# A vision stack on one Trainium2 core: transposes and projections of a chunked scan in one matmul per half

## The chip, the cores and the metric

The kernel runs on one core of a Trainium2 chip. The time is the device time of that core, in microseconds (us), for one execution over a batch of eight images. The engines have these names: PE (TensorE) multiplies matrices and writes to PSUM, with its weight loads shown apart as PEld; DVE (VectorE), ACT (ScalarE) and POOL (GpSimd) work on elements; SP issues DMAs. [...]

## The reference, cut to what matters

The input is x of shape (8, 64, 64, 96). Four layers follow each other, each adding its output to its input: three state-space blocks (layers 0, 1 and 2) and a spectral layer. The change lies in layer 1. There the normalised input is projected to 192 inner channels, passed through a 3x3 depthwise convolution and silu (call the result u), and scanned in K = 4 directions: rows, columns, and both reversed. For every direction k and every position, a projection of u gives 6 values of dt, 16 of B and 16 of C. The scan goes by chunks:

```python
x_dbl = jnp.einsum('blkd,kcd->blkc', xs, x_proj_w)
dts, Bs, Cs = jnp.split(x_dbl, [R, R + D_STATE], axis=3)
dt = jax.nn.softplus(dts + dtb)
S_loc = jnp.einsum('bcsh,bcshn,bcshd->bchdn', decay_end * dtr, Brh, xr)
```

Here `xr` is u with positions first. So the chunked scan needs u, dt and B with positions on the partitions, where the convolution leaves u with channels on the partitions. Every value is fp32.

## The kernel before, in words

The images go one after the other. For each, `u` and `y` lie in SBUF as two halves of 96 channels, each with L = 4096 positions. Layer 1 is `chunked_scan`, which calls `chunked_order` (L744) twice: order 0 for rows (directions 0 and 2), order 1 for columns (directions 1 and 3). A call has two parts.

The first part is a block whose order of work on each engine is set by the Tile planner, from its own costs and the order of the source. In order 0 it begins with the convolution (L766 to L774), which is mostly DVE's work (L256, L258) with a last block on PE (L269); POOL scales the identity for that (L263). Then PE computes B and C of all positions with channels on the partitions (L782), DVE copies them out (L790) and SP writes them to memory (L793). Then comes the loop over NQ = 32 chunks of Q = 128 positions (L796 to L820). In order 1 a chunk of u is a strided view, so POOL and ACT first copy the two halves to `uc` (L802, L803), which has four buffers. For each half, PE transposes the 96 x 128 piece into the PSUM tile `pt`, two buffers (L807); ACT for even chunks and DVE for odd ones copies it to `xt` (L808). PE then multiplies the same two pieces with the projection's columns for dt and B of both directions, 2 x 22 = 44 columns, adding up the halves in the PSUM tile `px`, which holds four chunks in one buffer (L812); DVE copies it to `xd` every fourth chunk (L820). In both kinds of PE work the piece of u is the stationary operand, loaded as 128 columns. After the loop, DVE adds the bias to dt (L824), ACT takes softplus (L829), DVE multiplies by A (L834), PE sums along the chunk (L839), ACT takes exp (L840), and DVE forms `d_end` (L841). Each of these works on all chunks at once.

The second part, the main part, is the scan itself in an order written out by hand (L1064 to L1085), a step for every two chunks. It begins with the DMA loads of `bt` and `cr` on SP's queue (L863, L867) and PE's `pl` (L872), and its matmuls into `py` (L1022, L1030) are the last that it issues. Its tiles take over memory from those of the first part.

## Time and profile before

| what | value |
|---|---|
| median of 3 runs | 31217.13 us (31208.32 to 31267.33) |
| profiled execution | 31126.95 us, its span 31125.2 us |
| PE, weight loads | 24477.4 us (79%), 9300.6 us (30%) |
| DVE | 24790.2 us (80%) |
| ACT | 16342.4 us (53%) |
| POOL | 21609.0 us (69%) |
| mean granted TensorE clock | 0.732 |

A line of the groups reads: source line, engine, operation, tile written and tiles read, partitions x elements, count; then total busy us and mean ns of one; then the engine's idle us just before these instructions, and what ended it. A line of the timeline reads: start, length in us, engine, line, operation, how many were merged. A line of the stretches is explained where it stands. L numbers are lines of the kernel before. "PEclk" or the granted clock is the share of full speed at which TensorE was let run.

### The profile page before, as it was taken

Reading aid. Unit: us, or ns where it says so; the run is one execution under the profiler, and the core shown is the slowest. Engines: PE = TensorE matmul, PEld = TensorE weight load, DVE = VectorE, ACT = ScalarE, POOL = GpSimd, SP = SyncE. Lnnn points to the kernel's source line nnn. Section 1 sums busy time; section 2 is a strip of 40 time slices with the busy share of each in tenths; the row PEclk is TensorE's granted clock in tenths of the full one; section 3 lists DMA queues with packets and bytes.
Section 4 is the critical chain, followed back from the end, with each engine's and each line's share of the span. In section 5 each row is a group of like instructions: output and inputs, shape, how many; then the busy total and the mean of one; then the engine's idle time right before and its main releaser. Section 6 shows DMA issues by size and latency. Waiting matters only on the chain. (4 is left out here: it accounts for less than half of the span.)

```text
span 31125.2 us, 279248 instructions
## 1 busy us (share of the span) xinstructions
PE 24477.4 (79%) x90246; PEld 9300.6 (30%) x90246; DVE 24790.2 (80%) x17921; ACT 16342.4 (53%) x28493; POOL 21609.0 (69%) x8844
## 2 busy tenths in 40 slices
PE   7797877978779787797877978779787797877978
PEld 1241422414225132241412414124141241412414
DVE  9859688596885968859698596985969859698596
ACT  5536455364553645536455364653646536465364
POOL 8739487395873958739587394973948739487394
PEclk7777776777777777777777777777777777776777
DMA  5315253052530525305253152531525315253152
GB/s 124 90 24 131 64 120 92 23 133 64 119 93 21 131 67 120 92 23 132 64 122 89 25 132 63 123 88 28 133 59 123 88 27 132 60 123 88 27 132 62
DMA packets 1503971, 2689.39 MB, mean 86 GB/s; under 512 B 305624, under 2 KB 313144, under 8 KB 1502512
## 3 DMA queue, kind: packets, MB, share of 16 engines
q1 hardware_dynamic: 1485872, 2665.23, 36.6%
q8 instruction: 722, 11.83, 0.2%
q10 hardware_dynamic: 16640, 6.29, 0.1%
q14 instruction: 737, 6.04, 0.1%
HBM read 2287.51 MB, written 383.06 MB: 86 GB/s over the span
## 5 line engine op out<-in xcount | busy, mean ns | idle before, releaser
L569 DVE TENSOR_TENSOR_SCAN h<-da,db 128x1026 f32<-128x1026 f32 x6144 | 13727.8, 2280 | 513.0 <-PE py L607 173.9
L590 POOL TENSOR_TENSOR h<-h,c 128x2048 f32<-128x2048 f32 x3072 | 12755.2, 4183 | 148.4 <-ACT state L585 144.5
L533 PE MATMUL pu<-du,cst 32*128 32x512 f32 x4096 | 3239.1, 881 | 3525.3 <-DVE db L539 3493.7
L554 ACT ACTIVATE da<-dx,a0s 128x512 f32<-128x512 f32 x6144 | 4235.3, 690 | 2600.4 <-DVE h L569 2440.4
L554 ACT ACTIVATE da<-dx,a2s 128x512 f32<-128x512 f32 x6144 | 4234.5, 690 | 2591.4 <-DVE h L569 2432.0
L607 PE MATMUL py<-h,cst 128*32 128x512 f32 x24576 | 5432.2, 814 | 68.3 <-POOL h L590 68.0
L539 POOL TENSOR_TENSOR db<-du,b 128x2048 f32<-128x2048 f32 x1024 | 4657.7, 4549 | 580.8 <-ACT db L525 580.8
L539 DVE TENSOR_TENSOR db<-pu,b 128x2048 f32<-128x2048 f32 x2048 | 4637.4, 2264 | 6.3 <-issue 6.3
L607 PEld LDWEIGHTS py<-h,cst 128*32 128x32 f32 x24576 | 1182.6, 145 | 4982.1 <-issue 4505.5
L533 PEld LDWEIGHTS pu<-du,cst 32*128 32x128 f32 x4096 | 802.3, 243 | 5542.4 <-DVE db L539 3998.6
L229 POOL TENSOR_SCALAR xn<-xs,sb 96x512 f32<-96x512 f32 x192 | 208.0, 1088 | 3179.8 <-DVE sb L209 3038.8
L455 PE MATMUL pv<-u,wk 96*128 96x512 f32 x2048 | 1765.1, 1003 | 759.0 <-ACT raw L451 759.0
L952 ACT ACTIVATE sg<-sg 128x768 f32<-128x768 f32 x1024 | 819.2, 800 | 2422.4 <-PE sg L936 2422.4
L883 POOL TENSOR_TENSOR rr<-lr,cc 128x768 f32<-128x768 f32 x256 | 435.9, 1703 | 2266.9 <-ACT lr L881 1177.4
L446 PE MATMUL pv<-u,wk 96*96 96x512 f32 x2048 | 1475.4, 849 | 501.1 <-ACT state L585 239.4
L597 PE MATMUL py<-y,cst 96*96 96x512 f32 x1536 | 1551.2, 1108 | 394.6 <-ACT raw L460 356.7
L498 POOL TENSOR_TENSOR du<-raw,u 96x512 f32<-96x512 f32 x1024 | 1445.7, 1438 | 0.0
L984 DVE TENSOR_TENSOR wt<-wt,cbm 128x768 f32<-128x768 f32 x1024 | 1091.0, 1085 | 344.5 <-ACT wt L953 341.2
L585 ACT COPY state<-h 128x4 f32<-128x4 f32 x3072 | 604.6, 197 | 1163.9 <-DVE h L569 1163.8
L1022 PE MATMUL py<-wt,xdt 128*32 128x128 f32 x12288 | 1017.0, 331 | 233.2 <-DVE y L1060 155.0
L1146 DVE SCALAR_TENSOR_TENSOR f<-p,w3bs,f 128x512 f32<-128x512 f32 x768 | 576.4, 751 | 718.6 <-ACT f L1139 691.8
L1030 PE MATMUL py<-ce,state 96*96 96x128 f32 x3968 | 1115.4, 371 | 0.0
(210 smaller groups left out, 32236.4 us busy)
## 6 DMA issues: line engine op xcount, KB each, us to landing
dx<-dd SPq DMA_DIRECT2D x4096, 192.0 KB, 3.8
b<-bcd SPq DMA_DIRECT2D x2048, 256.0 KB, 5.2
c<-bcd SPq DMA_DIRECT2D x2048, 256.0 KB, 6.5
du<-dud SPq DMA_DIRECT2D x2048, 128.0 KB, 2.7
dd<-raw SPq DMA_DIRECT2D x1024, 192.0 KB, 5.3
dud<-du SPq DMA_DIRECT2D x512, 128.0 KB, 1.9
xd<-xs SPq DMA_DIRECT2D x256, 192.0 KB, 2.1
xs<-xd SPq DMA_DIRECT2D x128, 384.0 KB, 5.8
```

What stands on the lines that cost most here:

```text
L446: nc.tensor.matmul(pv[:DM], weights[k][:, hi, 128:], uv[hi], start=(hi == 0), stop=(hi == 1))
L455: nc.tensor.matmul(pv, weights[k][:, hi, :128], uv[hi], start=(hi == 0), stop=(hi == 1))
L498: nc.gpsimd.tensor_mul(cut(du[:, hf, :], wh), cut(delta[hf], wh), uv[hf])
L533: nc.tensor.matmul(pu, sel[rows, :], m["du"][rows, n // 3, :], start=True, stop=True)
L539: (nc.gpsimd if pool else nc.vector).tensor_mul(groups(m["db", n]), (m["du2"][:, n // 3, :] if pool else m["pu"]) .unsqueeze(1) .to_broadc ...
L554: nc.scalar.activation(dst[:, g, :LC], made[i]["dx"][n // 3][:, n % 3, :], AF.Exp, scale=av4[:, k, n, gs : gs + 1],)
L569: nc.vector.tensor_tensor_scan(made[i]["h", n][:, at][:, way], das[p][:, rev : 2 * SEG + rev][:, way], made[i]["db", n][:, at][:, way], 0. ...
L590: nc.gpsimd.tensor_mul(h, h, made[i]["c"])
L597: nc.tensor.matmul(py, skip[:, hf, :] if k == 0 else ident[:DM, :DM], view((u if k == 0 else y)[:, hf, :], wh, c * LC, LC), start=True, st ...
L607: nc.tensor.matmul(py[32 * q : 32 * q + 32, :], red, hs[q][:, g, :], start=False, stop=(g == NSG - 1),)
L984: nc.vector.tensor_mul(it["wt"], it["wt"], m["cbm"][:, j : j + 1, :].to_broadcast([128, RK, Q]),)
L1030: nc.tensor.matmul(py[:, i, hf, :], it["before"][:, 96 * hf : 96 * hf + 96], m["ce"][:, j, :], start=False, stop=True,)
```

## The change

In the loop over chunks, each half of a chunk gets one matmul in place of a transpose and a projection matmul. Its moving operand `tx` holds, side by side, the 96 x 96 identity and that half's 44 columns of the projection: 140 columns. POOL builds `tx` once per order, in four copies. The result goes to a PSUM tile `pt` of 2 x 140 columns[...], with three buffers; `px` is gone. The transposed piece is copied to `xt` as before, from two runs of 96 columns. The two halves of dt and B are no longer added in PSUM: ACT copies the first half's 44 columns to `xd`, and DVE adds the second half's, for every chunk.

```diff
+        TX = DM + 2 * (RK + NST)
...
-            tc.tile_pool(name="pt", bufs=2, space=PSUM) as ptp,
-            tc.tile_pool(name="px", bufs=1, space=PSUM) as pxp,
+            tc.tile_pool(name="pt", bufs=3, space=PSUM) as ptp,
...
+            tx = cp.tile([DM, 2, TX], F32, name="tx", bufs=1)
+            for hf in range(2):
+                nc.gpsimd.tensor_copy(tx[:, hf, :DM], ident[:DM, :DM])
+                nc.gpsimd.tensor_copy(
+                    tx[:, hf, DM:].rearrange("p (i r) -> p i r", i=2),
+                    xproj[:, o::2, hf, : RK + NST],
+                )
...
-                pt = ptp.tile([128, 192], F32, name="pt")
+                pt = ptp.tile([128, 2, TX], F32, name="pt")
                 for hf in range(2):
-                    nc.tensor.transpose(pt[:, hf * 96 : hf * 96 + 96], uv[hf], ident[:DM, :DM])
-                (nc.vector.tensor_copy if c % 2 else nc.scalar.copy)(xt[:, c, :], pt)
-                if c % 4 == 0:
-                    px = pxp.tile([128, 4, 2, RK + NST], F32, name="px")
-                for hf in range(2):
-                    nc.tensor.matmul(
-                        px[:, c % 4, :, :],
-                        uv[hf],
-                        xproj[:, o::2, hf, : RK + NST],
-                        start=(hf == 0),
-                        stop=(hf == 1),
-                    )
-                if c % 4 == 3:
-                    nc.vector.tensor_copy(xd[:, c - 3 : c + 1, :, :], px)
+                    nc.tensor.matmul(pt[:, hf, :], uv[hf], tx[:, hf, :], start=True, stop=True)
+                (nc.vector.tensor_copy if c % 2 else nc.scalar.copy)(
+                    xt[:, c, :].rearrange("p (j m) -> p j m", j=2), pt[:, :, :DM]
+                )
+                xdc = xd[:, c, :, :].rearrange("p i r -> p (i r)")
+                nc.scalar.copy(xdc, pt[:, 0, DM:])
+                nc.vector.tensor_add(xdc, xdc, pt[:, 1, DM:])
```

## The prediction

> **What bounds the kernel now.** I read the engine table first: PE 79%, DVE 80% and POOL 69% of the span, so no one engine bounds the whole, and the change touches one stage: the loop over 32 chunks that precedes the chunked scan's main part. It runs twice per image (order 0 over rows, order 1 over columns), 16 times in the span. The groups show its members:

> ```profile
> L812 PE MATMUL px<-w1s,uc 96*128 96x44 f32 x1024 | 215.4, 373 | 0.0
> L812 PEld LDWEIGHTS px<-w1s,uc 96*128 96x128 f32 x1024 | 214.8, 302 | 0.0
> L807 PEld LDWEIGHTS pt<-cst,uc 96*128 96x128 f32 x512 | 102.5, 245 | 46.6 <-POOL uc L802 32.8 <-issue 13.5
> L803 ACT COPY uc<-u 96x128 f32<-96x128 f32 x256 | 119.7, 482 | 183.5 <-PE px L812 111.3 <-PE py L1030 67.9 <-PE pt L807 0.7
> L808 DVE COPY xt<-pt 128x192 f32<-128x192 f32 x256 | 90.6, 356 | 418.9 <-PE pt L807 418.4
> L808 ACT COPY xt<-pt 128x192 f32<-128x192 f32 x256 | 80.6, 315 | 347.2 <-PE pt L807 340.0 <-issue 7.3
> L820 DVE COPY xd<-px 128x176 f32<-128x176 f32 x128 | 43.4, 339 | 37.9 <-PE px L812 37.3
> ```

> The reader is to see that everybody waits for PE here, and that one fp32 matmul is two records (1,024 for 512 matmuls) where a transpose is one. So a chunk has six weight loads of 128 columns: two for transposes, four for px. Then busy time by stretches of the first image: the conv before the loop, order 0's loop in three pieces, order 1's in two, then three stretches of the spectral layer:

> ```profile
> 1425.00:1434.40 9.40, 9.40 (x27) 3.15 (x26) 9.40 (x9) 3.44 (x4) 0.82 (x1) 1.00 0.01 2
> 1489.06:1495.09 6.03, 5.78 (x55) 5.25 (x53) 2.65 (x8) 1.59 (x5) 0.00 (x0) 1.00 0.10 26
> 1495.09:1506.48 11.39, 11.21 (x58) 10.62 (x59) 2.34 (x7) 1.28 (x4) 0.00 (x0) 0.51 0.24 58
> 1506.48:1517.00 10.52, 10.34 (x54) 9.76 (x55) 2.11 (x6) 1.59 (x5) 0.00 (x0) 0.50 0.00 0
> 1800.20:1807.06 6.86, 5.86 (x55) 5.39 (x53) 2.83 (x8) 4.89 (x13) 3.64 (x8) 0.92 0.15 39
> 1807.06:1818.90 11.84, 11.30 (x57) 10.78 (x58) 2.85 (x8) 5.06 (x13) 4.08 (x9) 0.50 0.10 26
> 3600.00:3605.00 5.00, 5.00 (x26) 5.00 (x25) 1.70 (x2) 1.29 (x2) 0.00 (x0) 0.50 0.00 0
> 3700.00:3740.00 40.00, 39.94 (x235) 29.15 (x234) 17.74 (x26) 17.57 (x25) 0.00 (x0) 1.00 0.00 1
> 3860.00:3880.00 20.00, 20.00 (x94) 20.00 (x94) 2.46 (x3) 3.07 (x3) 0.00 (x0) 0.50 0.00 1
> ```

> Columns: length, then busy us of PE, weight loads, DVE, ACT, POOL, then the granted clock. Weight loads fill 90% of the loop, ACT and DVE are a quarter busy (ACT 43% in order 1), and about 6 us into the loop the clock falls from 1.00 to 0.50 and stays there. The timeline gives the periods:

> ```profile
> 1501.59 1.01 PEld L812 LDWEIGHTS px<-w1s,u 96*128 96x128 f32 x4
> 1504.64 1.89 PEld L812 LDWEIGHTS px<-w1s,u 96*128 96x128 f32 x8
> 1506.26 0.37 PEld L807 LDWEIGHTS pt<-cst,u 96*128 96x128 f32 x1
> ```

> Four chunks repeat from a load like the last line at 1501.38 to this one: 4.89 us, 1.22 us a chunk. At clock 1.00 it was 0.59 (loads at 1489.57 and 1490.16). Order 1 takes 0.65 a chunk early and 1.26 late. From the first transpose after the bcd matmuls to the last xd copy, the trace's starts and ends give 29.9 to 30.8 us in order 0, mean 30.2 (28 chunks; four run earlier, under the conv), and 36.6 in order 1 (32 chunks): 8 x 66.8 = 534 us, 1.7% of the span. Nothing runs beside it: dt, softplus, pe and d_end need all of xd, the main part needs them.

> [...] 64x64 weights streaming without a pause (L1116, at 3600) got 0.50, 128x128 weights with 64 moving columns per load of 128 (L1169, at 3860) 0.50, but the conv's 96x96 weights without a pause (L269, at 1425) 1.00: as shares of the array at work an estimated 25%, 50% and 56%. The loop now: four matmuls of 44 columns against six loads of 128, well below. [...] the px loads are 0.11 us apart at full clock, 0.21 at half[...]

> **The change, part by part.** Removed per chunk: two transposes and two px matmuls, six loads. Added: two matmuls, four records, each 128 columns loaded and 140 moving. In the conv, records of 504 columns follow each other every 0.42 us at full clock, 0.833 ns a column: 140 x 0.833 = 0.117 us, just over the 0.111 of a load, which therefore hides, as loads do in the conv. PE per chunk: 4 x 0.117 = 0.47 us at full clock (was 0.59), 0.93 at half (was 1.22). The activity becomes 96 of 128 rows x nearly all the time, about 70%: above the conv, so I expect full clock where PE sets the pace.

> Evacuation: the xt copy stays (ACT 0.315 or DVE 0.356, though its source is now two runs of 96). Added is an ACT copy of 44 columns: not in the trace; bounded by ACT's 4-column state copy (0.197) and 192 columns (0.315): I take 0.22. And a DVE add of 44: 176 and 512 columns cost 0.339 and 0.683, so 0.16 + 44 x 1.02 ns = 0.20. Gone is DVE's 0.339 per four chunks. Sums per chunk: ACT 0.38, DVE 0.38, below PE. But the steps form a chain: matmuls 0.47 and 0.2 until the last has drained (a record of 0.286 against a spacing of 0.11), xt copy 0.32 or 0.36, xd copy 0.22 [...], add 0.20, four hand-overs at an estimated 0.07 (DVE's dt add to ACT's softplus took 0.04): 1.7 us. Three pt buffers make 0.57 a chunk. The floor is PE's 0.47; if ACT and DVE, in order, take turns (xt, xd, add, xt, xd: 0.32 + 0.22 + 0.20 + 0.36 + 0.22 = 1.32 for two chunks), 0.66. I take 0.62. In order 1 ACT also has the uc copy (0.447 apart when back to back): 0.447 + 0.38 = 0.83, below PE at half clock (0.93); at this pace the activity is near 40%, so half clock will come and go. Bounds 0.72 (ACT's copies overlap at their ends, as an xt and a uc copy started 0.22 apart now) to 1.1 (both uc copies inside the turns: (1.32 + 0.89)/2); I take 0.93.

> Early chunks: with every chunk needing a DVE add, and DVE in the conv until 1484, three pt buffers allow three instead of four. Order 0: 29 x 0.62 + 1.0 to drain = 19.0, against 30.2: -11.2. Order 1: 32 x 0.93 + 1.2 = 31.0 against 36.6: -5.6. Tail: the Softplus table load (1.28 us) sits behind ACT's last copy; it was issued at 1517.02 and hidden by PE (DVE's xd copy ended at 1518.91). Now ACT's last copy comes 0.2 before the add, and add plus two dt adds (0.82) cover it only in part: +0.5 per order. Sum: (-11.2 - 5.6 + 1.0) x 8 = -126 us.

> At nothing: tx, four POOL copies an order (an estimated 1.5 us by L802's 0.46 for 128 columns). In order 1 POOL is free at 1788.2 and the first transpose comes at 1800.2, after 12 us of bcd matmuls; the uc copies queued behind tx need 2.1. In order 0 it queues behind lw's copy, which ends at 1425.8, 8 us before the first chunk. Without that cover: 1.5 x 16 = 24 us. tx also holds its memory to the last matmul; if cr comes to lie there, order 0's cr DMAs move from 1497 to the loop's end, with bt's later ones behind them on SP. Order 1 has that already (cr at 1836.46), and its end-of-xd to d_end takes the same 6.4 us: nothing.

> The profiled execution took 31126.95 (span 31125.2), 90 below the median shown, 31217.13. The difference goes on the median: 31217 - 126 = 31091.

> **Rivals.** *Half clock stays*: 29 x 0.93 + 1.0, less the 6 us at full clock that the entry gives (about 6 x 0.46/0.47 = 6) = 22; order 1 32 x 0.95 + 1.2 = 31.6: (-8.2 - 5.0 + 1.0) x 8 = -98, 31119. For it: the present loop; against: the conv at 1.00. *The main part's clock moves*: from d_end to the last py matmul, order 0 takes 249.6 to 262.4 (mean 256.9), order 1 283.0 to 293.4 (mean 289.4), for equal work, by where half-clock stretches fall. If a shifted start gave all the long values: 5.5 x 8 + 4.0 x 8 = +76, total -50, 31167; all the short: -58 - 51 = -109, 30982. Nothing in the profile says which. *ACT pairs well in order 1* (0.72): 24.2, -12.4 instead of -5.6: -180, 31037. *Slower: the chain is not overlapped*. If the planner's order leaves one pt in flight (ACT's next copy queued behind one that waits for DVE), 1.7 us a chunk: 29 x 1.7 = 49 and 32 x 1.7 = 54, +19 and +18, x 8 = +296, 31513. It decides from 1.03 us a chunk in order 0 and 1.12 in order 1. Against it: ACT, DVE and POOL run ahead freely now, and three buffers have to be lost, not one.

> **How the numbers follow.** Forecast 0.45; half clock 0.17; good pairing or short main parts 0.15; long main parts or a slower order that eat the gain to within 62 us 0.14; chain serial, wholly or enough to lose, 0.09. A measurement tells about 0.2%, 62 us, from no change. Faster by more: nearly all of the first three, 0.75; same 0.15; slower 0.10. The range takes in good pairing with short main parts in one order, -225 (30990), and the half clock with long main parts, near -25 (31190); the likeliest case alone is 31040 to 31140.

> **What would show it.** PE's loop records: four of 96x140 per chunk, loads hidden. Clock near 1.00 in order 0's loop (else the half-clock rival). Loop lengths near 19 and 31 us. ACT's 44-column copy near 0.22, DVE's add near 0.20, with waits on each other; if PE waits for DVE's add longer than 0.5 us a chunk, the serial rival holds. The prediction is wrong if the 16 main parts change by more than the loops, or if the conv gets longer because adds are slotted into it.

## The result and the profile after

The changed kernel takes 30914.5 us in the median (30896.96 to 31024.2) beside 31208.32 us before: a ratio of 0.9913, 95% interval 0.989 to 0.9936. Measured again beside the experiments, it was 30943.04 against 31163.21, ratio 0.9934 (0.992 to 0.9949). So it is faster by about 0.7 to 0.9%, some 220 to 294 us. The profiled executions differ by 230 us (span 31125.2 before, 30895.2 after). The forecast was 126 us, its range began at 30990, and both measurements lie below it.

The groups of the loop in the changed kernel, in the columns used before (L815 is now the matmul, L816 the xt copy, L820 and L821 the copy and the add to xd, L810 ACT's uc copy):

```profile
L815 PE MATMUL pt<-tx,uc 96*128 96x140 f32 x1024 | 147.2, 292 | 17.2 <-DVE xd L821 16.7
L815 PEld LDWEIGHTS pt<-tx,uc 96*128 96x128 f32 x1024 | 129.6, 189 | 46.6 <-POOL uc L809 26.9 <-issue 16.6
L810 ACT COPY uc<-u 96x128 f32<-96x128 f32 x256 | 101.3, 450 | 69.2 <-PE py L1031 69.2
L821 DVE TENSOR_TENSOR xd<-xd,pt 128x44 f32<-128x44 f32 x512 | 92.6, 198 | 177.4 <-ACT xd L820 101.1 <-PE pt L815 45.4 <-POOL uc L809 27.7
L820 ACT COPY xd<-pt 128x44 f32<-128x44 f32 x512 | 91.2, 203 | 75.4 <-DVE xt L816 75.4
L816 DVE COPY xt<-pt 128x192 f32<-128x192 f32 x256 | 89.9, 351 | 16.5 <-PE pt L815 16.5
```

Four weight loads a chunk are left, and their mean fell from the 302 ns of px's loads to 189 at the same 128 columns. That goes with the clock: in the kernel before, px's loads were 0.11 us apart at 1.00 and 0.21 at 0.50. PE now waits a little for DVE's add (17 us in all), and ACT's 44-column copy for DVE's xt copy of the same pt (75 us). The stretches of the two loops of the first image, in the columns explained before, two lines of the kernel before and two of the changed kernel:

```profile
1489.06:1518.95 29.89, 28.88 (x170) 27.01 (x168) 7.81 (x23) 5.75 (x15) 0.00 (x0) 0.61 0.11 27
1800.21:1836.74 36.53, 33.78 (x195) 31.84 (x192) 9.56 (x26) 17.96 (x45) 12.72 (x28) 0.58 0.06 16
1491.80:1510.80 19.00, 16.11 (x118) 14.64 (x116) 9.90 (x46) 8.29 (x44) 0.00 (x0) 1.00 0.13 31
1797.60:1819.10 21.50, 18.36 (x131) 16.18 (x128) 10.61 (x50) 17.43 (x77) 11.99 (x28) 1.00 0.06 15
```

In the changed kernel the clock is 1.00 through both loops, in all eight images, where its mean had been near 0.60 and 0.58. Order 0's loop went from 30.2 to 19.0 us on the average, order 1's from 36.6 to 21.5. The starts and ends of instructions in the two traces, summed over eight images, put the 230 us here:

| stretch | before | after | difference |
|---|---|---|---|
| order 0's loop | 241.6 | 152.3 | -89.4 |
| order 1's loop | 292.8 | 172.1 | -120.7 |
| dt to d_end, both orders | 102.1 | 105.1 | +3.0 |
| main parts, both orders | 4380.8 | 4394.5 | +13.7 |
| spectral layer | 2679.3 | 2640.3 | -39.0 |
| all else | 23401.3 | 23403.9 | +2.6 |

The loops carry -210. The spectral layer has no line changed. It takes about 325 or about 344 us per image, and the stretches of two images of the changed kernel show the clock beside it:

```profile
3565.60:3890.20 324.60, 309.58 (x1761) 235.96 (x1762) 125.32 (x178) 118.27 (x162) 5.19 (x7) 0.90 0.05 12
15130.40:15473.70 343.30, 328.66 (x1760) 253.62 (x1761) 125.19 (x178) 118.29 (x162) 5.25 (x7) 0.85 0.04 11
```

The work is the same, the clock is 0.90 or 0.85. Most of the difference is one row of 192 matmuls without a pause between them. In the first and the third image of the kernel before:

```profile
3596.60 40.12 PE L1116 MATMUL pt<-filters,xt 64*64 64x128 f32 x192 [1.34 <-DVE xt L1111]
11397.97 21.98 PE L1116 MATMUL pt<-filters,xt 64*64 64x128 f32 x192 [1.34 <-DVE xt L1111]
```

The mean clock was 0.52 over the first of them and 1.00 over the second. Four images before, two after and four in the second profile of the changed kernel were long, so those 39 us are not the change's.

### The profile page after: what moved, and what is told of

It reads as the page before. It is cut to its first block, busy times and chain, and to the rows that moved or that the text cites. A ratio compares the mean times of both kernels' runs of the same rounds, so it can differ in the third digit from the quotient of the medians.

```text
span 30895.2 us, 278432 instructions
## 1 busy us (share of the span) xinstructions
PE 24193.8 (78%) x89222; PEld 9034.7 (29%) x89222; DVE 24821.1 (80%) x18305; ACT 16397.5 (53%) x29005; POOL 21602.0 (70%) x8908
```

## Experiments

Three theories of the 210 us: **A**, PE now streams for a larger share of the time, and that alone keeps the clock at 1.00; **B**, the transposes made it fall; **C**, fewer weight loads made the loop shorter. Mean loops over the eight images of each kernel's profile, in us, and ratios to the kernel before:

| kernel | order 0 | order 1 | ratio (95%) |
|---|---|---|---|
| before | 30.2 | 36.6 | 1 |
| after | 19.0 | 21.5 | 0.9913 (0.989 to 0.9936) |
| matmul split | 36.9 | 44.7 | 1.0022 (1.0011 to 1.0034) |
| before, px of 128 columns | 20.5 | 23.8 | 0.9899 (0.9883 to 0.9915) |
| after, two pt buffers | 25.4 | 28.7 | 0.9963 (0.995 to 0.9977) |
| change in order 0 alone | 19.0 | 36.6 | 0.9982 (0.9973 to 0.999) |
| after, again | 19.0 | 21.5 | 0.9934 (0.992 to 0.9949) |
| after, one reader per pt | 14.0 | 18.3 | 0.9926 (0.9914 to 0.9939) |
| after, four pt buffers | 15.4 | 17.7 | 0.9912 (0.9898 to 0.9926) |
| after, uc copies on ACT | 19.0 | 26.4 | 0.996 (0.9945 to 0.9976) |

### The kernel before, streaming more

```diff
+            wx = cp.tile([DM, 2, 128], F32, name="wx", bufs=1)
...
-                    px = pxp.tile([128, 4, 2, RK + NST], F32, name="px")
+                    px = pxp.tile([128, 4, 128], F32, name="px")
...
-                        px[:, c % 4, :, :],
+                        px[:, c % 4, :],
                         uv[hf],
-                        xproj[:, o::2, hf, : RK + NST],
+                        wx[:, hf, :],
```

wx holds the 44 columns of the projection and then 84 columns of the identity, whose products nothing reads.

> The kernel before, with transposes and six weight loads a chunk as they were, but the px matmuls stream 128 columns in place of 44 (84 of them columns of the identity that nothing reads)[...]. At full clock 128 columns take 0.107 us and hide under a load of 0.111, so PE's time is not longer. Theory A (share of the array at work keeps the clock): 4 x 0.107 in 0.59 us on 96 of 128 rows is 54%, the clock stays at 1.00, loops near 18.5 us (order 0, before 29.9) and 22 us (order 1, before 36.6), some 200 us faster than before with not one load fewer. Theories B (transpose mode makes the clock fall) and C (fewer loads make the gain): the clock still falls to 0.50 and the loops stay at 30 and 36.6 us, no change within 0.2%.

It does 84 columns of needless work per matmul, and takes 1.0% less time. The clock stayed as theory A said. The loops are longer than the 18.5 and 22 us expected, 20.5 and 23.8: about 0.69 us a chunk in order 0, where the first chunks of the kernel before took 0.59 at full clock, so the added columns did not hide entirely (0.10 us a chunk more). The stretches of its two loops in the first image:

```profile
1490.60:1511.10 20.50, 19.54 (x170) 18.21 (x168) 7.99 (x22) 5.61 (x15) 0.00 (x0) 1.00 0.11 28
1776.10:1799.80 23.70, 22.94 (x195) 20.88 (x192) 9.05 (x25) 17.47 (x45) 12.77 (x28) 1.00 0.05 14
```

PE's count of records is that of the kernel before (170 and 195, 168 and 192 loads), at clock 1.00 in place of 0.61 and 0.58, in all 16 loops. B falls, since the transposes are still there. The spectral layer says the same: in the first image of the kernel before, PE did nothing but transposes (L1108) in these 6.8 us. They had begun at 3587.28, after a pause of 5.7 us, and the clock rose:

```profile
3587.75:3591.16 3.41, 3.41 (x24) 3.41 (x23) 2.63 (x5) 0.00 (x0) 3.41 (x6) 0.50 0.48 121
3591.16:3594.57 3.41, 3.34 (x37) 2.72 (x35) 3.34 (x8) 0.00 (x0) 1.34 (x2) 1.00 0.02 5
```

It rose during these transposes in every image of all ten profiles (before and after: 3.7 to 6.9 us after the first, 16 of 16). C explains little: the loops lose 180.4 us (163.9 + 190.1 against 241.6 + 292.8) with not one load fewer, the changed kernel's 210.1. Its main parts of order 0 took 245 to 247 us in every image, 97 us less in all than before. Its loop does not explain that, and it helps its ratio.

### The matmul of the change, split in two

```diff
-                    nc.tensor.matmul(pt[:, hf, :], uv[hf], tx[:, hf, :], start=True, stop=True)
+                    nc.tensor.matmul(pt[:, hf, :DM], uv[hf], tx[:, hf, :DM], start=True, stop=True)
+                    nc.tensor.matmul(pt[:, hf, DM:], uv[hf], tx[:, hf, DM:], start=True, stop=True)
```

> The changed kernel with each half's one matmul of 140 columns split in two regular matmuls, of 96 (identity) and of 44 (dt and B), same pt tile and same evacuation. Eight weight loads a chunk in place of four, the same 4 x 140 columns streamed. If the clock follows the share of the array at work (theory A), 0.47 us of streaming in 8 x 0.111 = 0.89 us of loads is 39% of the array, the clock falls to 0.50 and a chunk takes 8 x 0.213 = 1.71 us: loops near 46 us (order 0) and 53 us (order 1), in all some 250 us slower than the kernel before. If it was the transpose mode that made the clock fall (theory B), it stays at 1.00 and a chunk takes 0.89 us: 27 and 30 us, some 75 us faster than before. If only the count of loads at the old half clock matters (theory C), 1.71 us as in A.

Neither number held alone. Order 0's loop in the first and the fourth image:

```profile
1491.00:1531.40 40.40, 39.50 (x234) 39.31 (x232) 11.40 (x46) 8.66 (x44) 0.00 (x0) 0.64 0.06 14
13173.10:13200.40 27.30, 26.42 (x234) 26.21 (x232) 11.31 (x45) 8.63 (x44) 0.00 (x0) 0.99 0.06 14
```

The same instructions take 27.3 us where the clock stays and 40.4 where it falls. It stayed in two of the eight loops of order 0 and in none of order 1: with 0.47 of 0.89 us of streaming, 52%, it mostly falls. (The kernel before streams 25% of a chunk at full clock without its transposes and 52% with them, and fell in 16 of 16 loops. So no run here shows whether the columns of a transpose count in full.) So the merging pays in two ways: half the loads (19.0 us in order 0 where the split takes 27.3 at clock 0.99), and the share of streaming that this leaves (75% against 52%).

### The change with two pt buffers

```diff
-            tc.tile_pool(name="pt", bufs=3, space=PSUM) as ptp,
+            tc.tile_pool(name="pt", bufs=2, space=PSUM) as ptp,
```

> The changed kernel with two pt buffers in place of three. If the chain matmuls, xt copy, xd copy, add sets the pace (1.83 us a turn, 0.61 x 3), a chunk takes 0.92 us at full clock: loops near 28.5 us (order 0) and 31 us (order 1) against 19.0 and 21.5. Theory A adds that 0.47 us of streaming in 0.92 us is 38% of the array, so that the clock falls to 0.50, the turn becomes 2.4 us and a chunk 1.2: loops near 34 and 39 us, no faster than the kernel before. If PE sets the pace, the loops stay at 19 and 21.5.

Its two loops of the first image:

```profile
1490.30:1515.70 25.40, 18.98 (x122) 15.36 (x120) 11.89 (x47) 8.40 (x46) 0.00 (x0) 0.99 0.09 22
1799.70:1828.40 28.70, 19.93 (x131) 16.44 (x128) 12.64 (x50) 18.19 (x77) 11.94 (x28) 1.00 0.05 11
```

The loops are 6.4 and 7.2 us longer with one buffer less, so a buffer's turn does set the pace; it came out 7 to 12% shorter than I reckoned (less 1.2 to drain, 0.81 us a chunk in order 0 and 0.86 in order 1; expected 0.92). The clock did not fall, at 0.467 of 0.81 to 0.86 us of streaming, 54 to 58%. My measure in shares of the array (38%) said that it would, and is wrong: it puts this loop below the split one's 39%.

### The change in order 0 alone

```diff
+                if o == 0:
+                    pt = ptp.tile([128, 2, TX], F32, name="pt")
...
+                else:
+                    pt = ptp.tile([128, 192], F32, name="pt")
```

> The change in order 0 alone; order 1 keeps transposes, px and its six loads (its tx is built and not read). If the two loops gain each for itself: order 0's loop 19.0 us, order 1's 36.6 us, so 8 x 11.2 = 89 us less in the loops than before and some 90 us off the whole, give or take the 50 to 80 us by which main parts and spectral layer differ between executions. If order 1's loop is faster because it is entered differently, it falls below 36 us here too.

Order 0's loops lose 89.6 us, order 1's stay (292.9 against 292.8): each order gains for itself. The whole fell by 0.18% (0.1 to 0.27%), near 56 us, less than the loops; its profile shows 17.6 us more in the main parts than that of the kernel before, and 18.7 less in the spectral layer. The difference between 56 and 90 is within what these stretches do by themselves.

### The changed kernel again, and the chain

> The changed kernel once more, beside the versions below. The same work with the same loops (19.0 and 21.5 us), 210 us less in the loops than before; the ratio to the kernel before between 0.989 and 0.9936. The spectral layer, which no line of the change touches, should again show two lengths per image (near 325 and near 344 us), and the number of long ones should differ from the first profile's two, if it is chance.

The loops repeat to 0.1 us (152.2 and 172.0 us summed). The main parts of order 0 were 269, 262, 251, 262, 249, 268, 265 and 249 us, where the first profile had 268, 272, 254, 256, 256, 262, 246 and 256.

The timeline of the changed kernel in order 0, one turn of four chunks:

```profile
1497.56 2.20 PE L815 MATMUL pt<-tx,u 96*128 96x140 f32 x16 [0.30 <-DVE xd L821]
1497.82 0.20 ACT L820 COPY xd<-pt 128x44 f32<-128x44 f32 x1 [0.55 <-DVE xt L816]
1498.05 0.20 DVE L821 TENSOR_TENSOR xd<-xd,pt 128x44 f32<-128x44 f32 x1 [0.26 <-ACT xd L820]
1498.31 0.32 ACT L816 COPY xt<-pt 128x192 f32<-128x192 f32 x1 [0.29 <-PE pt L815]
1498.53 0.20 ACT L820 COPY xd<-pt 128x44 f32<-128x44 f32 x1
1498.76 0.20 DVE L821 TENSOR_TENSOR xd<-xd,pt 128x44 f32<-128x44 f32 x1 [0.51 <-PE pt L815]
1498.88 0.35 DVE L816 COPY xt<-pt 128x192 f32<-128x192 f32 x1
1499.26 0.32 ACT L816 COPY xt<-pt 128x192 f32<-128x192 f32 x1 [0.54 <-PE pt L815]
...
1500.06 0.36 PE L815 MATMUL pt<-tx,u 96*128 96x140 f32 x1 [0.30 <-DVE xd L821]
```

PE does four chunks (16 records) in about 1.9 us, then waits for DVE's add; 2.50 us a turn, 0.625 a chunk. The first ACT line waited 0.55 us until DVE's xt copy had ended. Two versions loosen this. In one, ACT or DVE alone reads a chunk's pt, and DVE adds the halves of four chunks from SBUF:

```diff
+                copy = nc.vector.tensor_copy if c % 2 else nc.scalar.copy
+                copy(xt[:, c, :].rearrange("p (j m) -> p j m", j=2), pt[:, :, :DM])
+                copy(xh[:, c, :, :], pt[:, :, DM:])
+                if c % 4 == 3:
+                    nc.vector.tensor_add(
+                        xd[:, c - 3 : c + 1, :, :].rearrange("p c i r -> p c (i r)"),
+                        xh[:, c - 3 : c + 1, 0, :],
+                        xh[:, c - 3 : c + 1, 1, :],
+                    )
```

> The changed kernel with each chunk's pt read by one engine alone: ACT for even chunks, DVE for odd ones, copies xt and then both halves of dt and B (2 x 44 columns) to SBUF; DVE adds the halves of four chunks at a time. The chain loses two hand-overs[...]. If that chain makes the 0.61 us a chunk, PE's 4 x 0.119 = 0.48 remains: order 0's loop 29 x 0.5 + 1.2 = 15.7 us (now 19.0), order 1's near 20 (now 21.5, uc copies then close to the bound), so some 35 to 40 us off the whole, less than the main parts move. If PE's own spacing or the uc copies set the pace, the loops stay.

In the other, pt has four buffers and the convolution's acc one:

```diff
-            tc.tile_pool(name="pt", bufs=3, space=PSUM) as ptp,
+            tc.tile_pool(name="pt", bufs=4, space=PSUM) as ptp,
...
-            tc.tile_pool(name="acc", bufs=2, space=PSUM) as acp,
+            tc.tile_pool(name="acc", bufs=1, space=PSUM) as acp,
```

> The changed kernel with four pt buffers[...]. If the chain of one buffer's turn (1.83 us) makes 0.61 us a chunk with three, four give 0.48, PE's bound: order 0's loop near 15.5 us with four chunks early, order 1's near 20. If ACT and DVE taking turns (0.6 a chunk by themselves) set the pace, a fourth buffer gives little: 18 to 19 and 21 us.

The first gives 14.0 and 18.3 us, 65 us less in the loops than the change (259.0 against 324.4): better than expected in order 0, since six chunks now run under the convolution. The second gives 15.4 and 17.7, but order 1's loop begins later, for the planner puts a chunk ahead of the bcd matmuls (those of B and C, L789 here). PE's timeline there:

```profile
1769.88 0.74 PE L1031 MATMUL py<-ce,state 96*96 96x128 f32 x2
1771.87 1.30 PE L815 MATMUL pt<-tx,uc 96*128 96x140 f32 x4 [1.25 <-POOL uc L809]
1773.10 13.94 PE L789 MATMUL pr<-u,w1s 96*32 96x512 f32 x64
```

From the end of order 0's main part to order 1's loop it now takes 16.35 us in place of 12.06. That costs 34 us over eight images and takes back all of order 1's gain (30 us). Both ratios, 0.9926 and 0.9912, overlap those of the change. So the chain over the buffers is the bound of the change's loops, but 65 us is less than what the main parts (+15 against the change) and the spectral layer (+68) moved in the same profile, and neither version is shown to be faster than the change.

### The pace that I had forecast for order 1

```diff
-                    nc.gpsimd.tensor_copy(cut(uc[:, 0, :], True), view(u[:, 0, :], True, c * Q, Q))
+                    nc.scalar.copy(cut(uc[:, 0, :], True), view(u[:, 0, :], True, c * Q, Q))
```

> The changed kernel with both halves' uc copies on ACT in order 1, none on POOL; order 0 as it is. ACT's slots per chunk (uc 0.33 twice, xt 0.11 on the average, xd 0.09) make 0.87 to 0.95 us: order 1's loop 29 to 32 us, against 21.5 with one copy. This is the pace that the forecast gave order 1. Streaming is then 0.47 of 0.9 us, 52%, as in the split version: if the clock goes by that share, it falls to 0.50 in part of the images, and order 1's loops differ from image to image; if not, they all stay near 30 at clock 1.00.

Order 1's loop in the first and the second image:

```profile
1795.30:1821.00 25.70, 20.55 (x131) 17.06 (x128) 11.06 (x49) 24.34 (x105) 0.00 (x0) 1.00 0.05 12
5659.60:5690.10 30.50, 28.17 (x131) 26.75 (x128) 11.84 (x50) 25.86 (x105) 0.00 (x0) 0.59 0.04 11
```

Even with two uc copies a chunk ACT needs 25.7 us: again I had priced it too high (29 to 32). Less 1.2 to drain, that is 0.77 us a chunk, 61% of it streaming, more than with two pt buffers, and yet the clock did not always stay. In two images it was 0.50 for one stretch of 3.41 us and came back (a mean of 0.93). In the second image it fell to 0.50 (a mean of 0.59) and did not come back before the end, and the loop took 30.5 us, near the 31.0 of the forecast. A part of that loop:

```profile
5668.70:5685.80 17.10, 17.10 (x74) 16.89 (x72) 6.36 (x27) 15.17 (x62) 0.00 (x0) 0.50 0.01 1
```

At this clock a record took 0.231 us (17.10 over 74) where it takes 0.119 at 1.00, so PE was busy without a pause here, for 17 us, and the clock still stayed at 0.50. All 160 loops of these ten profiles begin at 1.00. So the runs show what keeps a full clock that is there. Whether a fallen one comes back is not settled by streaming alone: in two images it did, here it did not.

## Why the prediction was wrong

**What held.** The bound (weight loads on PE at half clock, engines behind waiting for PE) was read rightly. PE's 0.47 us a chunk at full clock: records follow each other every 0.119 us, 0.48. ACT's 44-column copy at 0.22 and DVE's add at 0.20: 0.203 and 0.198. Three early chunks: twelve records before the bcd matmuls' end, three chunks. ACT's 44-column copy and DVE's add wait on each other's work: the copy for DVE's xt copy of the same pt (75.4 us of ACT's idle time), the add for ACT's copy (101.1 us of DVE's). The chain over three buffers at 0.62 a chunk: 0.625 in the timeline, and order 0's loop 19.0 us as forecast. The full clock in order 0 held.

**The step that failed: "I take 0.93" for order 1.** It measured 0.63 (21.5 less 1.25 to drain, over 32). This term is 9.5 us an order, 76 us in all, and with it the loops' sum becomes -210. Two parts of the step were off. First, ACT's 0.83 (0.447 + 0.38). The 0.447 was a distance from start to start of uc copies in the kernel before, but the 0.38 were the durations of half an xt copy and an xd copy. In the changed kernel an ACT instruction starts 0.09 us after the start of an xd copy of 0.20, 0.22 after that of an xt copy of 0.32, and 0.32 to 0.38 after that of a uc copy of 0.45; that is about 0.54 a chunk, and ACT is busy 17.43 of 21.5 us. So ACT does not bound order 1. The chain over the pt buffers does, as in order 0: with two, three and four buffers order 1's loop took 28.7, 21.5 and 17.7 us. The forecast had this chain at 0.62 for order 0 and did not carry it over.

Second, the clock: I let it "come and go" in order 1 by a share of the array near 40%. At 0.63 a chunk PE streams three quarters of the time, and the clock never fell. That measure rested on two misreadings of the trace. L1116's 64x64 weights at 3600 were taken to show that 25% of the array gives 0.50, but the same row ran at 1.00 in four of the eight images. And the old loop's share was taken from its four matmuls of 44 columns alone, without the transposes. No trace shows that they may be left out; in the kernel before, the clock rose from 0.50 to 1.00 while PE did nothing but L1108's transposes. The full clock of order 0 was forecast by the same measure. More streaming at the same loads did keep it (px of 128 columns: at 1.00 in 16 of 16 loops, where it fell in 16 of 16 before), but the measure itself failed on the version with two buffers; that it gave the right answer here was in part luck. The forecast's own lower bound, 0.72 with a total of -180, was the nearest, and still too slow.

**Smaller terms.** The tail of +0.5 per order: the table load did end after the dt adds (1511.82 against 1511.42 in the first image), but dt to d_end grew by 0.4 us in order 1 and by nothing in order 0, +3 us for 8. tx took POOL 0.96 us an order (2 x 0.262 + 2 x 0.216) for the 1.5 estimated, hidden both times. Order 0's loop begins 3.7 us sooner in all.

**The rivals.** Half clock stays: not in any loop of the changed kernel. The serial chain: no, three buffers overlap, though with two the loops are already 6.4 and 7.2 us longer. The main part's clock moves: the main parts did differ from image to image, and in the first profile were worth +14 us, but the spectral layer has it as well, -39 us there, which I had not counted. (The mean of order 0's main parts before is 258.2 us in the trace, not 256.9, so the long case would have been +66 and the short one -120.) The range's lower end took in 0.72 a chunk in order 1, where 0.63 was measured; that is 22 us. The rest of the distance to the measured times is of the size by which stretches without a changed line differ.

**The reason under the number.** I counted 20% fewer PE us at equal clock as a good part of the gain. At full clock the old loop takes 0.59 and 0.65 us a chunk, the new one 0.625 and 0.63: nearly nothing is won there, and a loop with all its loads but more streaming gets 180 of the 210 us.

## What to carry to other kernels

Before counting a PE stage's instructions, look at its granted clock: this stage, with four matmul records of 44 columns and two transposes behind six loads of 128 columns a chunk, ran at a mean clock near 0.60, and with 128 columns in place of 44, 84 of them useless, at 1.00. Look at a stage in every repetition before reading a rule off its clock: one image of L1116 misled the forecast. Price a busy engine by the distance from start to start of like neighbours in the trace, not by durations. And where stages with no line changed have two lengths, sum the stretches before crediting the whole difference to the change.

## What the runs showed of the hardware

| loops | share streaming | clock |
|---|---|---|
| before | 25%, with transposes 52% | fell in 16 of 16 |
| matmul split | 52% | fell in 14 of 16 |
| two pt buffers | 54 to 58% | stayed in 16 of 16 |
| uc copies on ACT, order 1 | 61% | stayed in 5 of 8, dipped in 2, fell in 1 |
| before, px of 128 columns | 61 to 62%, with transposes 83 to 85% | stayed in 16 of 16 |
| the change | 74 to 75% | stayed in 16 of 16 |

The share alone isn't the rule: the copies on ACT stream more than two buffers do and hold the clock less well. Whether time or the number of columns per weight load decides is not separated either, for the split changes both.

What comes just before goes with it too. L1116's 192 matmuls with 64x64 weights always start at 1.00. Either the clock stays and they take 22.0 us, or it falls to 0.50 within 3 us (1.30 to 2.79 in the profiles before and after), does not come back before their end, and they take 39 to 40. The clock records of these two profiles show 1.00 and 0.50 alone, in stretches that each last a multiple of 3.41 us (3.41, 6.83, 10.24, 13.65 and longer; the last record of each profile apart). Counted from the changes of the clock in steps of 3.41 us, all L1116 rows of the ten profiles that start 0.6 to 2.2 us after a step are long, and all others short, 80 images without an exception; before and after, the six long ones start 0.63 to 2.11 us after a step, the ten short ones 0.05 to 0.54 or 3.20 to 3.23. So the two lengths of the spectral layer go with where its 1.34 us pause before L1116 falls. The split loop (27.3 or 40.4 us in order 0) and the main parts (246 to 272 us in order 0 of the changed kernel) do not sort themselves so simply by their start; why one is long, and what sets the border, stays open.
